# Three VectorE operations of a graph-attention kernel take one operand from PSUM instead of SBUF

## The chip, the cores and the metric

The kernel runs on one core of a Trainium2 chip. A core has five engines with a queue of instructions each: TensorE (PE), which multiplies 128 x 128 tiles and writes to PSUM; VectorE (DVE) and ScalarE (ACT), which work on 128 partitions at a time and reach SBUF and PSUM; GpSimd (POOL), which here issues the gathers and scatters whose row numbers lie in SBUF; and SyncE (SP), which issues plain transfers. Engines wait for each other through semaphores. The metric is the device time of one execution in microseconds (us). The kernel before took 1271.98 us, the median of three runs (1270.6 to 1276.46).

## The reference

6250 nodes with 256 features, 100,000 edges (src, dst), two attention heads of 128 features. The layer norm of the features is projected, each edge gets a weight, the weighted rows of the destinations are summed by source, and a feed-forward layer follows in which each row goes to the one expert of eight that its gate likes best:

```python
Wh = (x @ W_w + W_b).reshape(N, H, D)              # x: layer norm of the input
s = jnp.einsum('nhd,d->nh', Wh, a_src); t = jnp.einsum('nhd,d->nh', Wh, a_dst)
e = jax.nn.leaky_relu(s[src] + t[dst], negative_slope=0.2)
m = jax.ops.segment_max(e, src, num_segments=N)
ex = jnp.exp(e - m[src])
alpha = ex / jax.ops.segment_sum(ex, src, num_segments=N)[src]
agg = jax.ops.segment_sum(alpha[:, :, None] * Wh[dst], src, num_segments=N)
h_prime = jnp.where(deg[:, None, None] > 0, agg, Wh)
...
x = x + h_prime                                    # first residual
H = jax.nn.gelu(xf @ W1 + b1, approximate=False)   # xf: layer norm of x
probs = jax.nn.softmax(H @ Wg + bg); assign = jnp.argmax(probs, axis=-1)
out = x + probs[assign] * (H @ Wd[assign] + bd[assign])
```

## The kernel before

It works in a prelude and 49 blocks of 128 nodes (`NB`), the last of 106.

**Prelude, 0 to about 115 us.** Each partition gets 784 edges as keys made of source and destination, and VectorE sorts them (`exchange`, L290). Between the steps of the sort VectorE takes the layer norm's statistics, TensorE projects the nodes, and ScalarE writes a row of 260 numbers for each node to `table` in HBM: two heads of 128 features with the terms of the attention. The bias `Wb` is loaded to 128 partitions (L246). `hot_terms` (L491) takes the attention terms of the first 256 nodes, the "counted destinations", from `hot_x` into `hot_e`; edges to these nodes are not gathered but counted per pair of source and destination.

**Blocks.** A block takes three slots of time, and the work of several blocks overlaps. `at(slot, place, fn)` collects all work in a plan, and the sorted plan is the order in which every engine's queue is filled; no scheduler changes it. For block b with u = 3b, the pieces that matter here are:

- `window` (L615): POOL fetches the block's sorted keys. `measure` and `split` (L625, L657) on VectorE take counts, row numbers (`dsti`) and places from them. `split` has the two long operations that make `pick` (L662, L663).
- `pick_pairs` (L677), slot u-2, place 62.758: four comparisons (L681) make `dests`; L682 compares the row numbers 128 to 255, read from the bf16 tile `iota_bf`, with `place_i` and makes `places`, 128 x 512 bf16. TensorE multiplies the two into the counts of pairs (L691).
- `fetch` (L788), slots u to u+2, place 30: POOL gathers the rows of 5, 5 and 4 edges per partition, each in one indirect DMA of 128 rows (L792). The row number of each partition is read from `dsti` in SBUF. The tile `wg` has five buffers.
- `compare_back` (L806), slots u+1 to u+3, place 51.259: VectorE compares `iota_ps` with `loc` and makes the one-hot tile `hot` (L809). `iota_ps` holds the numbers 128 to 255 in fp32 in the PSUM tile `fix`.
- `weigh` (L814), slots u+2 to u+4, place 8.751: VectorE makes the factors (L821, L822), puts them into columns 128 to 183 of `fix`, multiplies the gathered rows for one head by them (L823); ScalarE copies the factors from `fix` (L824) and weighs the other head (L826).
- `add_up` (L828), slots u+3 to u+5: TensorE sums the gathered rows by source (L833).
- `scale_terms` on ScalarE (L704) and `weigh_pairs` on VectorE (L706), slot u+2, place 51: L709 takes the maximum of `wt` and one half of `hot_e`, and L710 multiplies by the counts in PSUM.
- `owned` and `owned_biased` (L797, L802), slots u+5 and u+6: the block's own rows of x are loaded, and L804 adds the bias to them. `finish` (L840) adds the sums of the edges.

Four blocks at a time go through the first half of the feed-forward layer (L920), are sent by POOL to lists by expert (L1064), and full tiles of a list come back for the second half (L1154). After the last block a tail of such tiles follows.

`fix` fills one PSUM bank of 512 fp32 columns: `iota_ps` in 0 to 127, the factors in 128 to 183, and nothing in the rest. VectorE writes and reads it, ScalarE reads it at L824. The planner of semaphores puts accesses of two engines to one PSUM bank in order, also where both read.

Of the kernel before, what the change touches and what calls it, by code (L numbers as in the profile page):

```python
# [10 lines left out]
F32 = mybir.dt.float32  # L11
# [3 lines left out]
AF = mybir.ActivationFunctionType  # L15
# [8 lines left out]
P = 128  # L24
# [12 lines left out]
def common_path(  # L37
# [22 lines left out]
    nc = tc.nc  # L60

    N, C = x.shape
    E = src.shape[0]
    HC = W.shape[1]
    D = a.shape[0] // 2
    H = HC // D
# [13 lines left out]
    HB, HK = 2, 4  # L80
# [5 lines left out]
    T = ND + NC  # L86
# [4 lines left out]
    D2 = D + H  # L91
    TW = H * D2
    SE = D2 + D
# [17 lines left out]
    const = ctx.enter_context(tc.tile_pool(name="const", bufs=1))  # L111
# [50 lines left out]
    iota_bf = const.tile([P, HOT], BF16, name="iota_bf")  # L162
    nc.vector.tensor_copy(iota_bf, iota_s[:, :HOT])

    hot_x = const.tile([P, HB, TW], F32, name="hot_x")
    hot_e = const.tile([P, HB, 2, H], F32, name="hot_e")
    cnt = const.tile([P, NB], F32, name="cnt")
    late = const.tile([P, NB, 3], F32, name="late")
    den_all = const.tile([P, NB, H], F32, name="den_all")
    nc.gpsimd.memset(den_all, 1.0)  # L170
    bad = const.tile([P, 4], F32, name="bad")

    bias = const.tile([P, C], F32, name="bias")
    src_term = const.tile([P, NB, H, 3], BF16, name="src_term")

    def rows_of(b):
        return min(P, N - b * P)
# [16 lines left out]
    with ExitStack() as edges:  # L194
# [3 lines left out]
        def at(slot, place, fn, *args):  # L198
            plan.append((slot, place, len(plan), fn, args))
# [9 lines left out]

        fix = pfix.tile([P, 512], F32, name="fix")  # L210
        iota_ps = fix[:, :P]
        nc.vector.tensor_scalar(iota_ps, iota_r, float(P), None, op0=ALU.add)

        pre = ExitStack()
        sp = pre.enter_context(tc.tile_pool(name="sort", bufs=1))
# [3 lines left out]
        def early(t, fn, *args):  # L219

            at((t - TG) / TS, 0, fn, *args)
# [21 lines left out]
                                in_=W[:, h * D:(h + 1) * D].rearrange("(k p) c -> p k c", p=P))  # L243
        a_bc = sp.tile([P, 2 * D], F32, name="a_bc")
        nc.scalar.dma_start(out=a_bc, in_=a.partition_broadcast(P))
        nc.scalar.dma_start(out=bias, in_=Wb.partition_broadcast(P))  # L246

        keya = sp.tile([P, KQ * P], F32, name="keya")
# [241 lines left out]

        def hot_terms():  # L491
            for g in range(HB):
                nc.vector.tensor_copy(hot_e[:, g], hot_x[:, g, :].rearrange("p (a c) -> p a c", a=2)[:, :, D:])
            nc.vector.memset(hot_x[:, :, D:D2], 1.0)

        def node_terms():
# [9 lines left out]
        early(0.25, make_keys)  # L506
        early(0.3, columns, KC)
        early(0.32, bias_terms)
        early(7, keep_gaps)
        NODE, XN0 = 1.6, 9.0  # L510
        for i, (d, flip) in enumerate(steps):
# [17 lines left out]
        for f0, f1, t0, step in ((n0, n1, 8.0, 0.7), (n4, NB - 1, 15, 2.0)):  # L529
            for j, b in enumerate(range(f0, f1)):  # L530
                c = b % CH
# [24 lines left out]
        early(TG - 0.5, node_terms)  # L556
        early(70, load_hot)
        early(76, hot_terms)


# [41 lines left out]
        wt = {}  # L602
# [10 lines left out]
        win, kept, rows, own, sums, res = {}, {}, {}, {}, {}, {}  # L613
# [63 lines left out]
        def pick_pairs(b):  # L677
            pair, place_i = kept[b].pop("pair"), kept[b].pop("place")
            d, p = kept[b]["both"] = [kp.tile([P, HK, w], BF16, name=n, bufs=1) for n, w in (("dests", HOT), ("places", P))]
            for r in range(HK):  # L680
                nc.vector.tensor_scalar(d[:, r, :], iota_bf, pair[:, r:r + 1], None, op0=ALU.is_equal)  # L681
            nc.vector.tensor_tensor(p, iota_bf[:, P:2 * P].unsqueeze(1).to_broadcast([P, HK, P]),  # L682
                                    place_i[:, :HK].unsqueeze(2).to_broadcast([P, HK, P]), op=ALU.is_equal)

        def count_pairs(b):
# [13 lines left out]
        def scale_terms(b, g):  # L699
            tm = kept[b]["tm"]  # L700
            if g == 0:
                kept[b]["wt"] = ep.tile([P, HB, H, P], F32, name="wt", bufs=2)
            for h in range(H):
                nc.scalar.activation(kept[b]["wt"][:, g, h, :], tm[:, h, :], AF.Identity, scale=hot_e[:, g, 1, h:h + 1])  # L704

        def weigh_pairs(b):  # L706
            kept[b].pop("tm")
            wt = kept[b]["wt"]
            nc.vector.tensor_max(wt, wt, hot_e[:, :, 0, :].unsqueeze(3).to_broadcast([P, HB, H, P]))  # L709
            nc.vector.tensor_mul(wt, wt, kept[b].pop("pc").unsqueeze(2).to_broadcast([P, HB, H, P]))  # L710

        def add_pairs(b):
# [88 lines left out]

        def owned_biased(b):  # L802
            r = rows_of(b)
            nc.vector.tensor_add(own[b][:r], own[b][:r], bias[:r])  # L804

        def compare_back(b, q):  # L806
            hot = ep.tile([P, HT, P], F32, name="hot", bufs=4)
# [390 lines left out]
        for b in range(NB):  # L1198
            u = 3 * b
            at(u + -6, 64.258, window, b)  # L1200
            at(u + -4, 24, measure, b)
            at(u + -4, 50.755, prefix, b)
            at(u + -3, 5, prefix_out, b)
            at(u + -3, 12, split, b)
            at(u + -3, 33.7, gather_late, b)
            at(u + -2, 62.758, pick_pairs, b)
            at(max(u + -1, -0.2), 63, load_terms, b)
            at(u + 1, 18.756, scale_terms, b, 0)
            at(u + 2, 4.751, scale_terms, b, 1)
            at(u + 0, 51.019, count_pairs, b)  # L1210
            at(u + 2, 51, weigh_pairs, b)
            at(u + 4, 51.256, add_pairs, b)
            at(u + -2, 16, choose, b)
            at(u + -2, 33.5, spread, b)
            at(u + 0, 9, compare, b)
            at(u + 0, 33, factors, b)
            at(u + 1, 47, factor_sums, b)
            at(u + 5, 42.752, owned, b)
            at(u + 6, 13, owned_biased, b)
            for q in range(3):  # L1220
                at(u + 0 + q, 30, fetch, b, q)
                at(u + 1 + q, 51.259, compare_back, b, q)
                at(u + 2 + q, 8.751, weigh, b, q)
                at(u + 3 + q, 32, add_up, b, q)
            at(u + 6, 14, finish, b)
# [3 lines left out]
        for k in range(NPH):  # L1229
# [19 lines left out]
            for i in range(len(bs)):  # L1249
                t, p = (((v + 6, 40), (v + 6, 41), (v + 8, 60), (v + 8, 61))[i] if last else  # L1250
                        ((v + 10, 38), (v + 11, 38), (v + 12, 21.26), (v + 13, 57.754))[i])
# [34 lines left out]
@with_exitstack  # L1286
def gat_then_ffn_kernel(
    ctx: ExitStack,
    tc: tile.TileContext,
    x: bass.AP,  # L1290
    src: bass.AP,
    dst: bass.AP,
    W: bass.AP,
    Wb: bass.AP,
    a: bass.AP,
    W1: bass.AP,
    b1: bass.AP,
    Wg: bass.AP,
    bg: bass.AP,
    Wd: bass.AP,  # L1300
    bd: bass.AP,
    out: bass.AP,
):
    keep = ctx.enter_context(tc.tile_pool(name="keep", bufs=1))
    odd = keep.tile([1, 1], I32, name="odd")
    common_path(tc, x, src, dst, W, Wb, a, W1, b1, Wg, bg, Wd, bd, out, odd)
    flag = tc.nc.values_load(odd[0:1, 0:1], min_val=0, max_val=1,
                             skip_runtime_bounds_check_because="a flag, 0 or 1")
    with tc.If(flag > 0):
        general_path(tc, x, src, dst, W, Wb, a, W1, b1, Wg, bg, Wd, bd, out)  # L1310
# [506 lines left out]
```

## Time and profile before

| | |
|---|---|
| time of three runs | 1270.6, 1271.98, 1276.46 us |
| the profiled execution's own time | 1270.99 us |
| its span, first to last instruction | 1268.9 us |
| outside the span | 2.1 us |
| mean granted TensorE clock | 0.948 of full speed |
| PE busy | 1108.0 us (87%) |
| VectorE busy | 969.4 us (76%) |
| POOL busy | 835.5 us (66%) |
| ScalarE busy | 677.6 us (53%) |
| gathers (L792) | 686, mean 981 ns |
| L682, L709, L804 on VectorE | 49 of each, mean 681, 685 and 418 ns |

Busy time is the time in which an engine carries out instructions; what it waits for, and what it needs between two instructions, is not in it. The view by line gives for a group of instructions the busy time, the mean duration, the idle time of the engine just before them and what ended it ("issue" where no wait of the profile ended just then). The view of windows gives busy times for a stretch of the span. A timeline row begins with the start in us from the span's start and the duration in us.

### The profile page before, as it was taken

What the parts mean: (1) busy time and instruction counts of PE and PEld (TensorE: products, weight loads), DVE (VectorE), ACT (ScalarE), POOL (GpSimd) and SP (SyncE); (2) the same over time, 40 slices, a digit from 0 to 9 for tenths busy, and PEclk for the clock granted to TensorE, in tenths of its full rate; (3) what the DMA queues carried; (4) which work ended last, traced back from release to release, by engine and by line L of the source; (5) the groups of instructions that cost most, each with busy time, mean ns of one, the idle gap of its engine ahead of it and who ended that gap; (6) DMA issues with size and microseconds to landing.
All of it is one profiled execution on the core that took longest, in us unless ns stands there. A gap on an engine that the chain in (4) does not pass through costs nothing.

```text
span 1268.9 us, 22698 instructions
## 1 busy us (share of the span) xinstructions
PE 1108.0 (87%) x6551; PEld 864.0 (68%) x6551; DVE 969.4 (76%) x3509; ACT 677.6 (53%) x2011; POOL 835.5 (66%) x941
## 2 busy tenths in 40 slices
PE   4685677697888989999989999999999999999994
PEld 3464565566566677786876867868678687685784
DVE  6986889888979789798897997979979979753110
ACT  4684344555646447556474665655745647555221
POOL 1003777777777777777777777777777777736551
PEclk9797688898998989999999999999999999999998
DMA  4764776656555666666766666575667566747860
GB/s 142 220 196 137 200 199 207 192 190 200 173 173 176 218 172 214 190 223 197 216 191 217 212 195 206 183 241 177 222 187 227 183 211 187 230 138 298 318 202 13
DMA packets 115977, 249.77 MB, mean 197 GB/s; under 512 B 23372, under 2 KB 69656, under 8 KB 115702
## 3 DMA queue, kind: packets, MB, share of 16 engines
q0 software_dynamic: 44192, 131.04, 33.3%
q1 hardware_dynamic: 64342, 110.14, 27.3%
q10 hardware_dynamic: 7312, 7.05, 1.7%
q8 instruction: 56, 0.92, 0.3%
q14 instruction: 75, 0.61, 0.2%
HBM read 196.90 MB, written 57.97 MB: 201 GB/s over the span
## 4 chain that ended last, share of the span: by engine, by line
PE 42%; DVE 25%; DMA 12%; ACT 10%; issue 5%; POOL 4%; SPq 0%; ACTq 0%; DVEq 0%; POOLq 0%
PE pf L1154 11%; PE p_a L833 10%; PE pf L920 9%; DMA wg<-table,dsti 7%; POOL wg L792 3%; DVE wg L823 3%; PE pm L738 3%; DVE hot L809 3%; PE pf L1043 2%; ACT wg L826 2%; DMA lbc<-lrow 2%; DVE pick L663 2%; PE pf L456 1%; PE p_a L717 1%; DVE dests L681 1%
## 5 line engine op out<-in xcount | busy, mean ns | idle before, releaser
L792 POOL DMA_INDIRECT wg<-table,dsti x686 | 672.8, 981 | 211.4 <-issue 162.5
L833 PE MATMUL p_a<-wg,hot 128*128 128x258 f32 x1372 | 339.8, 396 | 0.0
L833 PEld LDWEIGHTS p_a<-wg,hot 128*128 128x128 f32 x1372 | 265.9, 198 | 57.4 <-issue 17.9
L826 ACT ACTIVATE wg<-wg 128x128 f32<-128x128 f32 x686 | 216.7, 390 | 4.8
L1154 PE MATMUL pf<-wd_sb,half 128*128 x880 | 205.6, 387 | 1.1
L1154 PEld LDWEIGHTS pf<-wd_sb,half 128*128 128x128 f32 x880 | 163.3, 191 | 31.4 <-ACT half L1044 5.5
L920 PE MATMUL pf<-xT,w_sb 128*128 128x512 f32 (+1 forms) x416 | 182.4, 584 | 0.5 <-ACT xT L912 0.5
L824 ACT COPY wg<-fix 128x10 f32<-128x10 f32 x147 | 24.1, 164 | 224.9 <-DVE wg L823 188.6
L920 PEld LDWEIGHTS pf<-xT,w_sb 128*128 128x128 f32 x416 | 75.3, 196 | 73.3 <-issue 69.2
L1044 ACT COPY half<-pf 128x512 f32<-128x512 f32 x110 | 59.1, 588 | 115.2 <-PE pf L1043 115.2
L823 DVE TENSOR_TENSOR wg<-wg,fix 128x640 f32<-128x640 f32 x147 | 114.1, 776 | 5.1
L809 DVE TENSOR_TENSOR hot<-fix,loc 128x640 f32<-128x640 f32 x147 | 112.7, 767 | 0.0
L738 PE MATMUL pm<-rest,pick 128*128 128x33 f32 x588 | 82.3, 295 | 15.1 <-DVE place_i L666 15.0
L738 PEld LDWEIGHTS pm<-rest,pick 128*128 128x128 f32 x588 | 77.8, 211 | 16.0 <-ACT wg L826 9.8
L922 ACT ACTIVATE hT<-pf,b_sb 128x512 f32<-128x512 f32 (+1 forms) x104 | 65.7, 655 | 29.4 <-PE pf L920 28.3
L456 PE MATMUL pf<-w_sb,xT 128*128 128x260 f32 x196 | 61.6, 443 | 19.1 <-ACT xT L450 19.0
L1064 POOL DMA_INDIRECT by_expert<-row,place_i x47 | 48.4, 1030 | 37.4 <-ACT row L1059 19.9
L704 ACT ACTIVATE wt<-tm,hot_e 128x128 f32<-128x128 f32 x196 | 67.8, 395 | 0.0
L619 POOL DMA_INDIRECT win<-keys,first x49 | 46.9, 958 | 28.9 <-DMA keys<-keyb 12.0
L821 DVE TENSOR_TENSOR fe<-fs,wg 128x10 f32<-128x10 f32 x147 | 24.1, 164 | 53.9 <-DMA wg<-table,dsti 50.1
L1043 PE MATMUL pf<-ident,hT 128*128 128x128 f32 x392 | 54.4, 278 | 10.7 <-ACT row L1044 5.4
L456 PEld LDWEIGHTS pf<-w_sb,xT 128*128 128x128 f32 x196 | 38.6, 219 | 28.7 <-ACT xT L450 24.3
(273 smaller groups left out, 1800.1 us busy)
## 6 DMA issues: line engine op xcount, KB each, us to landing
row<-by_expert SPq DMA_DIRECT2D x39, 641.0 KB
lbc<-lrow SPq DMA_DIRECT2D x49, 448.0 KB
wg<-table,dsti POOLq DMA_INDIRECT x686
wg<-by_expert SPq DMA_DIRECT2D x16, 641.0 KB
wd_sb<-in_L_ffn_Wd_dram SPq DMA_DIRECT2D x8, 1024.0 KB
tm<-terms SPq DMA_DIRECT2D x49, 128.0 KB
table<-tb ACTq DMA_DIRECT2D x12, 520.0 KB
xs<-in_x_dram SPq DMA_DIRECT2D x12, 512.0 KB
```

Of the source, the lines that this page charges most:

```text
L456: nc.tensor.matmul(pW[:, :TW], xT[:, k * P:(k + 1) * P], w_sb[:, k, :], start=(k == 0), stop=(k == KC - 1))
L704: nc.scalar.activation(kept[b]["wt"][:, g, h, :], tm[:, h, :], AF.Identity, scale=hot_e[:, g, 1, h:h + 1])
L738: nc.tensor.matmul(pk[:, c, :], k["pick"][:, c * P:(c + 1) * P], k["rest"], start=True, stop=True)
L792: nc.gpsimd.indirect_dma_start(out=wg[:, t - QS[q], :], out_offset=None, in_=table[:, :], in_offset=bass.IndirectOffsetOnAxis(ap=kept[b][" ...
L809: nc.vector.tensor_tensor(hot[:, :n], iota_ps.unsqueeze(1).to_broadcast([P, n, P]), kept[b]["loc"][:, QS[q]:QS[q + 1]].unsqueeze(2).to_bro ...
L823: nc.vector.tensor_mul(wg[:, :, :D], wg[:, :, :D], p_w[:, :, 0:1].to_broadcast([P, n, D]))
L826: nc.scalar.activation(wg[:, t, D2:SE], wg[:, t, D2:SE], AF.Identity, scale=wg[:, t, D + 1:D2])
L833: nc.tensor.matmul(sums[b], hot[:, t - QS[q], :], wg[:, t - QS[q], :SE], start=(t == 0), stop=(t == T - 1))
L920: nc.tensor.matmul(ph[:, :w], wt["w1"][:, k, j * P:(j + 1) * P], xT[:, k, :w], start=(k == 0), stop=(k == KC - 1))
L922: nc.scalar.activation(hT[:, j, :w], ph[:, :w], AF.Gelu, bias=wt["b1"][:, j:j + 1])
L1043: nc.tensor.transpose(pT[:, j * P:(j + 1) * P], rows(4 * h + j), ident)
L1154: nc.tensor.matmul(py[:, :C], res[k]["half", i, j // 4][:, j % 4, :], wt["wd"][:, ds(of * KH + j * C, C)], start=False, stop=(j == KH - 1))
```

## The change

The free columns of `fix` take two more constants. Columns 184 to 187 become `hot_ps`, the one half of the counted destinations' terms; columns 256 to 511 become `bias_ps`. Then:

- L682 reads `iota_ps` (fp32, PSUM) in place of the upper half of `iota_bf` (bf16, SBUF). Its other input, `place_i`, and its output stay in SBUF.
- L709 reads `hot_ps` in place of `hot_e[:, :, 0]`.
- L804 reads `bias_ps` in place of `bias`.
- `hot_terms` makes four copies of 128 x 2 in place of two of 128 x 4; two of them go to PSUM.
- A copy of 128 x 256 from `bias` to `bias_ps` is added to the prelude, just after `bias_terms`; the SBUF tile `bias` is given up after the prelude.

The instructions of the other engines and their order are the same. On VectorE two waits for ScalarE move or appear: in the slots that have L709, the wait for ScalarE's read of `fix` (L824) that stood at L809 stands at L709, two operations earlier; and L804 waits for L824 too, which it did not.

```diff
+        hot_ps = fix[:, P + 2 * T * H:P + 2 * T * H + HB * H].rearrange("p (g h) -> p g h", h=H)
+        bias_ps = fix[:, 512 - C:]
...
             for g in range(HB):
-                nc.vector.tensor_copy(hot_e[:, g], hot_x[:, g, :].rearrange("p (a c) -> p a c", a=2)[:, :, D:])
+                nc.vector.tensor_copy(hot_ps[:, g], hot_x[:, g, D:D2])
+                nc.vector.tensor_copy(hot_e[:, g], hot_x[:, g, SE:])
...
         early(0.32, bias_terms)
+        early(0.33, lambda: nc.vector.tensor_copy(bias_ps, bias))
...
-            nc.vector.tensor_tensor(p, iota_bf[:, P:2 * P].unsqueeze(1).to_broadcast([P, HK, P]),
+            nc.vector.tensor_tensor(p, iota_ps.unsqueeze(1).to_broadcast([P, HK, P]),
                                     place_i[:, :HK].unsqueeze(2).to_broadcast([P, HK, P]), op=ALU.is_equal)
...
-            nc.vector.tensor_max(wt, wt, hot_e[:, :, 0, :].unsqueeze(3).to_broadcast([P, HB, H, P]))
+            nc.vector.tensor_max(wt, wt, hot_ps.unsqueeze(3).to_broadcast([P, HB, H, P]))
...
-            nc.vector.tensor_add(own[b][:r], own[b][:r], bias[:r])
+            nc.vector.tensor_add(own[b][:r], own[b][:r], bias_ps[:r])
```

More of the change, by code (lines that the diff above doesn't have):

```diff
@@ L165, in common_path @@
     hot_x = const.tile([P, HB, TW], F32, name="hot_x")
-    hot_e = const.tile([P, HB, 2, H], F32, name="hot_e")
+    hot_e = const.tile([P, HB, H], F32, name="hot_e")
     cnt = const.tile([P, NB], F32, name="cnt")
@@ L171, in common_path @@
     bad = const.tile([P, 4], F32, name="bad")
-    bias = const.tile([P, C], F32, name="bias")
     src_term = const.tile([P, NB, H, 3], BF16, name="src_term")
@@ L245, in common_path @@
         nc.scalar.dma_start(out=a_bc, in_=a.partition_broadcast(P))
+        bias = sp.tile([P, C], F32, name="bias")
         nc.scalar.dma_start(out=bias, in_=Wb.partition_broadcast(P))
@@ L703, in scale_terms @@
             for h in range(H):
-                nc.scalar.activation(kept[b]["wt"][:, g, h, :], tm[:, h, :], AF.Identity, scale=hot_e[:, g, 1, h:h + 1])
+                nc.scalar.activation(kept[b]["wt"][:, g, h, :], tm[:, h, :], AF.Identity, scale=hot_e[:, g, h:h + 1])
         def weigh_pairs(b):
```

## The prediction

> **What bounds the kernel now.** I read the busy times by window first, then POOL's waits, then the gathers' line, then timeline rows in which two engines meet.
>
> The page gives PE 87% and POOL 66%, which makes POOL look idle. The windows (length, then busy time and count of PE, PE's weight loads, VectorE, ScalarE and POOL, then clock, DMA share and GB/s) say how steady the blocks are:
>
> ```profile
> 115.00:320.00 205.00, 149.42 (x925) 118.96 (x925) 169.04 (x597) 92.19 (x307) 156.93 (x160) 0.82 0.65 193
> 520.00:720.00 200.00, 191.92 (x1222) 151.92 (x1221) 169.36 (x611) 113.58 (x335) 153.22 (x161) 0.99 0.66 207
> 920.00:1116.00 196.00, 189.03 (x1192) 147.72 (x1191) 161.29 (x577) 113.24 (x333) 149.71 (x157) 1.00 0.65 205
> ```
>
> POOL is busy about 153 us in 200 and carries out about 160 instructions in each. Its waits from 130 to 1110 us (total, times, longest) show what fills the rest:
>
> ```profile
> POOL wg L792 <- issue: 158.5, 520, 0.3
> POOL wg L792 <- DMA wg<-table,dsti: 10.4, 34, 0.3
> POOL wg L792 <- PE p_a L833: 8.8, 29, 0.3
> ```
>
> No gap before a gather is longer than 0.3 us, whoever is named, and nearly every gather has one: 158.5 / 520 = 0.30. It is a fixed cost between two of them, not a wait. 160 x 0.30 = 48 us, and 153 + 48 = 201 of 200: POOL works back to back from 115 to 1116 us. One gather costs 0.945 + 0.30 = 1.25 us. The gathers' own line tells the rest (min/median/max in ns, and who waited for them):
>
> ```profile
> L792 POOL DMA_INDIRECT wg<-table,dsti x686: 942/949/1497, 114.9 to 1116.3; - x172
> ...
>   DVE fe L821: 50.1, 18
>   ACT wg L824: 26.3, 8
> ```
>
> The consumers run up against the gathers 26 times, for 76 us; the times of these waits lie between 211 and 1089 us, the last one (ScalarE) 5.4 us long at 1089. PE and VectorE fall behind while a feed-forward group passes (the chain that ended last is then on PE), then catch up and wait for a gather's landing. So POOL's issue sets the pace of the 1001 us of blocks; PE, 192 of 200 in the middle, is close behind.
>
> **What holds a gather.** The median is 949 ns and the mean on the page 981. The timeline around 428 us (start, us):
>
> ```profile
> 428.08 0.68 DVE L682 TENSOR_TENSOR places<-iota_bf,place_i 128x512 bf16<-128x512 bf16 x1
> 428.12 1.48 POOL L792 DMA_INDIRECT wg<-table,dsti  x1 [0.30 <-issue]
> ...
> 430.76 0.68 DVE L709 TENSOR_TENSOR wt<-wt,hot_e 128x512 f32<-128x512 f32 x1
> 431.16 1.10 POOL L792 DMA_INDIRECT wg<-table,dsti  x1 [0.30 <-issue]
> ```
>
> The first gather starts 0.04 us after L682 and ends at 429.60, which is 0.84 us after L682's end (428.76). The second starts under L709 and ends at 432.26, 0.82 us after L709's end (431.44). Both behave as if the last 0.83 us could begin only when the VectorE operation was over: about 0.11 us after its start a gather needs something, its row numbers in SBUF I think, that the operation keeps from it.
>
> I counted this in the trace: for each of POOL's 839 indirect DMAs, which VectorE operation runs 130 ns after its start, and what the DMA takes above 945 ns. All excess is 31.1 us. Under L682: 25 DMAs, 6.6 us. Under L709: 25 DMAs, 5.1 us. Under L663 (two SBUF inputs, unchanged): 21, 6.7 us. Under L804: nothing, its place in the slot misses the reads. Under L809 (99 DMAs) and L710 (22), which read one operand from PSUM: 4 and 6 ns each, nothing. So an operation of the same size with one PSUM operand does not hold a gather, and that is what the change makes of L682 and L709.
>
> **The change part by part.**
>
> **1. Gathers released.** 6.6 + 5.1 = 11.7 us less POOL time. As a check from sizes: a 0.68 us operation meets a reading in 0.68 / 1.25 = 54% of 49 cases, that is 27, for 0.34 us on average, 9 us each; the trace has 25 and 25 and less per case. [...]
> A freed gather's successors start earlier and may run into L663, L662 or L771, which still hold. The unchanged holders cost 31.1 - 11.7 = 19.4 us in 1001, 2% of the time, so 0.2 us of 11.7 by chance; since POOL and VectorE are not independent I take 1.0. PE's nearness takes a tenth, 1.0. Left: 9.7 us, all on the path.
>
> **2. The operations' own time.** Rows of VectorE (busy, mean ns, idle before):
>
> ```profile
> L710 DVE TENSOR_TENSOR wt<-wt,pm 128x512 f32<-128x512 f32 x49 | 33.6, 686 | 1.7
> L709 DVE TENSOR_TENSOR wt<-wt,hot_e 128x512 f32<-128x512 f32 x49 | 33.6, 685 | 6.8 <-ACT wg L824 3.3 <-ACT wt L704 3.2
> L682 DVE TENSOR_TENSOR places<-iota_bf,place_i 128x512 bf16<-128x512 bf16 x49 | 33.3, 681 | 0.0
> L809 DVE TENSOR_TENSOR hot<-fix,loc 128x512 f32<-128x512 f32 x49 | 32.8, 670 | 0.0
> ```
>
> L710 takes 686 with an operand in PSUM where L709 takes 685 without; L809 is what L682 becomes but for the output's type, 670 against 681. L804 (128 x 256, 418 ns) has a pair of half its size: L747 from SBUF 359, L749 from PSUM 354. Sum: 49 x (-11 + 1 - 5) ns = -0.7 us. [...]
>
> **3. Prelude.** VectorE is busy without a break from 18 to 104 us there, and all else waits for the sorted keys, so its additions are on the path. The copy of 128 x 256 to PSUM: nearest are 0.39 for a 128 x 224 copy (L284) and 0.37 for a 128 x 256 cast (L163); 0.4. Two more small copies: a COPY of 128 x 4 is 179 ns (L1000), some 0.1 of it overlapped, and one new wait on VectorE itself; 0.25 (between 0.15 and 0.5). Sum +0.65.
>
> **4. Waits.** L709 now waits until ScalarE has done L824, which until now was asked two operations later. In the trace ScalarE was done 0.64 us ahead of L709 in the median; in 9 of 49 cases it was not done 60 ns ahead, in all 1.0 us short. For L804 the lead is 1.8 us or more except twice, 0.35 us short in all. Behind the waiting L709 on VectorE's queue stand L710, L809 and the next slot's L821 to L823, and for these TensorE waits with the sums of the pairs (L717) and of the gathered rows (L833). VectorE idles 31 of 200 us, so 1.35 us is covered; without the cover it is +1.35. I take 0.
> Row numbers for the gathers (L753) come from VectorE two slots ahead, so POOL does not wait for it.
>
> **Sum.** -9.7 + 0.65, and -0.7 of VectorE hidden: -9.0 us. From the profiled execution: 1271.0 - 9.0 = 1262.0. The median of the three runs is 1.0 above the profiled one, which would give 1263; the lowest run is 0.4 below it. I say 1262.5.
>
> **Rivals.** A measurement of this kernel tells about 0.5%, 6.4 us, from no change: faster means below 1265.6, slower above 1278.3.
> - **PE takes the pace.** From 520 us on PE is busy 192 in 200. If it were the real floor there, the gathers' gain after 520 (60% of 11.7, 7.0 us) would be lost, and 4.7 - 0.65 = 4 us stays: 1268. For it: long stretches of PE in the chain after 870. Against: consumers still wait 5.4 us for a gather at 1089, and 198 us per 200, which the gain asks for, is above 192.
> - **The change doesn't release the gathers**, because what holds them is not the second SBUF operand, or they run into L663 instead: 0 + 0.65, 1272.6. Against: L809 and L710 hold nothing.
> - **ScalarE's wait on L709 becomes the bound.** ScalarE's queue also has the feed-forward's 0.65 us activations in front of L824. If POOL's lead shrinks and L824 comes later in the slot, VectorE stands at L709 in each of 49 blocks. A block is 20.4 us with 3.2 of VectorE idle; a stall decides only beyond 3.2. With a stall of 3.5 us in each block VectorE sets the pace, the gathers' gain lies hidden behind it, the path grows by 0.3 x 49 = 15, and with the prelude the end is 1272.0 + 15 + 0.65 = 1287.6. Against: the shortfall today is 1.0 us in all.
>
> **Chances.** Forecast 0.70; PE takes the pace 0.13; nothing released 0.10; ScalarE's wait 0.07. Of the forecast 0.02 ends above 1265.6, and of the PE case 0.04 below: faster 0.68 + 0.04 = 0.72, same 0.02 + 0.09 + 0.10 = 0.21, slower 0.07. Range: the forecast's own is 1257 (all of 11.7 and 3 us more by better phase) to 1267; with the PE case and part of the third, 1256 to 1271.
>
> **What would show it.** Right: gathers' mean falls from 981 to about 966 ns, POOL's busy time by 11 us, the last gather starts at about 1107 in place of 1116.3; L682, L709 and L804 within 15 ns of before; no gathers above 1.1 us under L682 or L709; idle before L709 below 9 us. Wrong if the mean stays near 981 (not released, or L663 takes them), if POOL's gaps exceed 0.3 (it waits for others: PE), or if idle time before L709 grows by tens of us.

## The result and the profile after

The changed kernel takes 1262.02 us (median of 6 runs, 1261.49 to 1263.06), the kernel before 1271.34 beside it (6 runs, 1270.1 to 1276.46). The ratio is 0.9924, with a 95% interval from 0.9903 to 0.9945: faster by 0.55 to 0.97%. The forecast was 1262.5. The profiled execution of the changed kernel took 1262.07 us with a span of 1260.0, against 1270.99 and 1268.9 before, so the two traces differ by 8.9 us. Five of the experiments below ran on chips on which the kernel before itself takes 1690 to 1724 us, at a granted clock of 0.84 to 0.86 (0.94 to 0.96 elsewhere); they stand apart, at the end.

In the block part the line numbers are 4 higher than before: L682 is now L686, L709 is L713, L804 is L808, and the gathers are L796. The page of the changed kernel, busy times and the gathers' row:

```profile
PE 1102.2 (87%) x6551; PEld 861.3 (68%) x6551; DVE 968.5 (77%) x3512; ACT 677.1 (54%) x2011; POOL 828.1 (66%) x941
...
L796 POOL DMA_INDIRECT wg<-table,dsti x686 | 664.1, 968 | 209.0 <-issue 172.1
```

The mean of a gather has gone from 981 to 968 ns. POOL is busy 7.4 us less, VectorE 0.9 us less; PE, at a granted clock of 0.953 in place of 0.948, is busy 5.8 us less. The clock is not what made the kernel faster: the six executions of the changed kernel have 0.946 to 0.953, and the one at 0.946 is the fastest of them, 1261.49 us; 26 executions of the kernel before beside the first experiments have 0.943 to 0.955 and take 1267.5 to 1276.2. The gathers' own line (min/median/max in ns, first and last start in us) and who waits for them:

```profile
L796 POOL DMA_INDIRECT wg<-table,dsti x686: 942/946/1454, 114.5 to 1106.0; - x172
...
  ACT wg L828: 45.4, 12
  DVE fe L825: 44.5, 22
```

The last gather starts at 1106.0 us in place of 1116.3. The consumers still run up against the gathers, 34 times for 90 us, so POOL's issue still sets the pace. Its waits from 130 to 1103 us (total, times, longest) say the same, with nothing above the fixed 0.3 us in front of a gather:

```profile
POOL wg L796 <- issue: 168.5, 553, 0.3
POOL wg L796 <- DMA wg<-table,dsti: 7.6, 25, 0.3
...
POOL wg L796 <- PE p_a L837: 7.0, 23, 0.3
```

The timeline around 611 us shows the two places at which the prediction's first view of the mechanism stood (start and duration in us). A gather that starts 0.27 us into L686, and one that starts together with L713, each take 0.95 us. Had they ended 0.83 us after the operation's end, as the held ones did before, they would have taken 1.24 and 1.51:

```profile
611.15 0.68 DVE L686 TENSOR_TENSOR places<-fix,place_i 128x512 bf16<-128x512 f32 x1
611.42 0.95 POOL L796 DMA_INDIRECT wg<-table,dsti  x1 [0.30 <-issue]
...
613.92 0.95 POOL L796 DMA_INDIRECT wg<-table,dsti  x1 [0.30 <-issue]
613.92 0.68 DVE L713 TENSOR_TENSOR wt<-wt,fix 128x512 f32<-128x512 f32 x1
```

The changed operations by shape (busy us, mean ns, idle before):

```profile
L714 DVE TENSOR_TENSOR wt<-wt,pm 128x512 f32<-128x512 f32 x49 | 33.7, 687 | 1.7
L713 DVE TENSOR_TENSOR wt<-wt,fix 128x512 f32<-128x512 f32 x49 | 33.4, 681 | 6.0 <-ACT wg L828 5.8
L686 DVE TENSOR_TENSOR places<-fix,place_i 128x512 bf16<-128x512 f32 x49 | 33.3, 680 | 0.0
...
L808 DVE TENSOR_TENSOR own<-own,fix 128x256 f32<-128x256 f32 x48 | 20.2, 421 | 3.5 <-DMA own<-in_x_dram 3.3 <-ACT wg L828 0.2
```

They cost what they cost before (681, 685 and 418 ns), and the two waits for ScalarE come to 5.8 us at L713 and 0.2 us at L808.

**Where the 8.9 us went.** From the first gather's start to the last one's end POOL carries out 774 indirect DMAs. I split that length into 774 x 0.945 = 731.4 us, the DMAs' excess over that (the holds), the memsets, and the gaps between instructions. The numbers come from the instructions' times in each trace; us:

| | first gather | length | holds | memsets | gaps | span |
|---|---|---|---|---|---|---|
| before | 114.9 | 1002.3 | 28.8 | 4.0 | 238.0 | 1268.9 |
| after | 114.5 | 992.5 | 21.2 | 4.5 | 235.3 | 1260.0 |

The length falls by 9.8: 7.6 from the holds and 2.7 from the gaps, less 0.5 at the memsets. The start is 0.4 earlier, the tail after the last gather 1.3 longer; 9.8 + 0.4 - 1.3 = 8.9.

And the holds by what ran on VectorE 130 ns after a DMA's start (all 839 indirect DMAs; how many met the operation, how many of these took more than 1.02 us, and their excess over 0.945 us in all):

| VectorE's operation | before | after |
|---|---|---|
| places (L682, L686) | 25, 17, 6.6 us | 31, 0, 0.4 us |
| terms (L709, L713) | 25, 22, 5.1 us | 29, 0, 0.05 us |
| second operation of pick (L663, L667), unchanged | 21, 15, 6.7 us | 23, 20, 9.0 us |
| lbc (L771, L775), unchanged | 21, 5, 1.6 us | 25, 12, 4.5 us |
| everything else | 11.1 us | 9.6 us |
| all | 31.1 us | 23.5 us |

More gathers than before meet the two changed operations, and none is held. 11.2 us were released, and 5.3 us more than before were spent under pick and lbc.

The ends of the DMAs say the same in another way. All 39 that took more than 1.02 us under L682 and L709 end 0.82 to 0.86 us after that operation's end, as the two in the prediction's timeline do.

Two large inputs in SBUF are not all that holds, though. lbc (L771, L775) and the first operation of pick (L662, L666) are unchanged and have one large input each, with one number per partition as the second operand. They hold too: 8 of 19 DMAs took more than 1.02 us under L662, and 13 of 23 under L666. And lbc also holds the last part of a DMA that began before it. The rows are from the changed kernel:

```profile
822.45 1.24 POOL L796 DMA_INDIRECT wg<-table,dsti  x1 [0.30 <-issue]
822.88 0.68 DVE L775 TENSOR_SCALAR lbc<-lbc,iota_p 128x1792 bf16<-128x1792 bf16 x1
```

The gather ends at 823.69, 0.12 us after lbc. 12 DMAs do so before and 17 after, for 2.3 and 3.2 us, which the table counts under what ran at 130 ns ("everything else"). Such holds at the end are not seen with L682 and L709: 44 DMAs began 0.2 to 0.8 us ahead of one of these two and still ran when it did, and none took more than 1.02 us. Why one large input is enough in these two operations and not in L681 (128 x 256; before, 31 DMAs met it and none took more than 1.02 us) is open; so is what the DMA waits for, its row numbers being the prediction's guess.

### The profile page after: what moved, and what is told of

Its sections match the earlier page's. It is cut to its first block, busy times and chain, and to the rows that moved or that the text cites. A ratio compares the mean times of both kernels' runs of the same rounds, so it can differ in the third digit from the quotient of the medians.

```text
span 1260.0 us, 22750 instructions
## 1 busy us (share of the span) xinstructions
PE 1102.2 (87%) x6551; PEld 861.3 (68%) x6551; DVE 968.5 (77%) x3512; ACT 677.1 (54%) x2011; POOL 828.1 (66%) x941
## 4 chain that ended last, share of the span: by engine, by line
PE 46%; DVE 23%; DMA 10%; ACT 8%; issue 5%; POOL 5%; SPq 1%; ACTq 0%; DVEq 0%; POOLq 0%
PE pf L1158 12%; PE p_a L837 11%; PE pf L924 10%; POOL wg L796 4%; DMA wg<-table,dsti 4%; PE pm L742 4%; DVE wg L827 3%; PE pf L1047 3%; DVE hot L813 2%; PE p_a L721 2%; PE pf L962 2%; ACT wg L830 1%; DVE pick L667 1%; DVE dests L685 1%; ACT hT L926 1%
## 5 line engine op out<-in xcount | busy, mean ns | idle before, releaser
L796 POOL DMA_INDIRECT wg<-table,dsti x686 | 664.1, 968 | 209.0 <-issue 172.1
L828 ACT COPY wg<-fix 128x10 f32<-128x10 f32 x147 | 24.0, 163 | 212.4 <-DVE wg L827 163.7
L813 DVE TENSOR_TENSOR hot<-fix,loc 128x640 f32<-128x640 f32 x147 | 112.7, 767 | 0.0
L742 PEld LDWEIGHTS pm<-rest,pick 128*128 128x128 f32 x588 | 76.1, 207 | 14.9 <-ACT wg L830 9.4
L1047 PE MATMUL pf<-ident,hT 128*128 128x128 f32 x392 | 54.4, 278 | 10.7 <-ACT row L1048 5.4
L825 DVE TENSOR_TENSOR fe<-fs,wg 128x10 f32<-128x10 f32 x147 | 23.7, 161 | 45.4 <-DMA wg<-table,dsti 44.5
L1048 ACT COPY row<-pf 128x512 f32<-128x512 f32 x94 | 50.6, 582 | 13.8 <-PE pf L1047 13.5
```

What stands on the lines that cost most here:

```text
L742: nc.tensor.matmul(pk[:, c, :], k["pick"][:, c * P:(c + 1) * P], k["rest"], start=True, stop=True)
L796: nc.gpsimd.indirect_dma_start(out=wg[:, t - QS[q], :], out_offset=None, in_=table[:, :], in_offset=bass.IndirectOffsetOnAxis(ap=kept[b][" ...
L813: nc.vector.tensor_tensor(hot[:, :n], iota_ps.unsqueeze(1).to_broadcast([P, n, P]), kept[b]["loc"][:, QS[q]:QS[q + 1]].unsqueeze(2).to_bro ...
L1047: nc.tensor.transpose(pT[:, j * P:(j + 1) * P], rows(4 * h + j), ident)
L1048: nc.scalar.copy(o, pT)
```

## The experiments

My theory: an indirect DMA on POOL is held while VectorE runs an operation with both large inputs in SBUF (whatever else may hold it); the change takes that from two operations, and POOL's issue sets the pace, so the time follows. The rivals: the bias, or the operands' type, makes the difference; what holds is not the memory; or POOL does not set the pace any more.

### One part at a time

**Only the places.** The kernel before, with L682 alone changed:

```diff
-            nc.vector.tensor_tensor(p, iota_bf[:, P:2 * P].unsqueeze(1).to_broadcast([P, HK, P]),
+            nc.vector.tensor_tensor(p, iota_ps.unsqueeze(1).to_broadcast([P, HK, P]),
```

> The kernel before with one line changed: the places are compared with row numbers from PSUM. Theory (a second SBUF operand holds the gathers): the 6.6 us that gathers took too long under this operation go, the other holders stay and take about a third of that back, as they did in the whole change; 1271.3 - 4.4 = 1267, the operation itself 680 ns as before, no gather above 1.1 us under it. Rival (the gain comes from moved waits or from the prelude, which this kernel leaves alone): 1271.

Measured: 1265.64 us (6 runs) beside 1272.27 (26 runs), ratio 0.9943 (0.9925 to 0.9961), that is -6.6 us. In its trace 25 gathers meet L682 and their excess is 0.30 us in all (6.6 before); 24 meet L709, which still has two inputs in SBUF, and lose 5.4. The sum of the holds in POOL's stretch is 24.4 us, 4.4 below before, and the gaps are 3.5 us shorter. This one edit has most of the gain, and it leaves the prelude and the two moved waits alone, so these don't make it.

**Only the terms.** The kernel before with `hot_ps`, its copies and L709 alone (here L711):

```diff
+        hot_ps = fix[:, P + 2 * T * H:P + 2 * T * H + HB * H].rearrange("p (g h) -> p g h", h=H)
...
-            nc.vector.tensor_max(wt, wt, hot_e[:, :, 0, :].unsqueeze(3).to_broadcast([P, HB, H, P]))
+            nc.vector.tensor_max(wt, wt, hot_ps.unsqueeze(3).to_broadcast([P, HB, H, P]))
```

> The kernel before with the counted destinations' terms in PSUM alone. Theory: 5.1 us of held gathers go, a third comes back, 0.3 us for two more copies in the prelude; 1271.3 - 3.1 = 1268. Rival (moved waits): this is the operation whose wait for ScalarE moves ahead, so it has either the whole gain of 9 us, 1262, or a loss of up to 1.4 us, 1272.7. Rival (no effect of PSUM): 1271.6.

Measured: 1270.2 us (8 runs), ratio 0.999 (0.9973 to 1.0007): -2.1 us, and not told from no change. The mechanism is there all the same: 24 gathers meet L711 with 0.01 us of excess, against 20 of 24 held under the places (6.1 us). But pick's second operation holds 10.1 us in this trace and lbc 4.3, so the holds in all fell by only 1.8 us.

**Only the bias.** The kernel before with `bias_ps`, its copy in the prelude and L804 alone:

```diff
+        early(0.33, lambda: nc.vector.tensor_copy(bias_ps, bias))
...
-            nc.vector.tensor_add(own[b][:r], own[b][:r], bias[:r])
+            nc.vector.tensor_add(own[b][:r], own[b][:r], bias_ps[:r])
```

> The kernel before with the bias in PSUM alone, with its copy in the prelude and its new wait for ScalarE. Theory: no gather was held under this operation, so nothing is won, and the copy costs 0.4 us; 1271.7. Rival (any operation with two SBUF inputs costs in proportion to its time, 418 ns against 681): a gain of about 3 us, 1268.

Measured: 1272.8 us (11 runs), ratio 1.0005 (0.9988 to 1.0022): nothing, as the theory has it for an operation that one DMA met in the kernel before, without being held. This trace is the most useful control of all. Nothing is released in it, and yet its holds are 37.1 us against 31.1 before: pick 11.1 where before had 6.7, lbc 5.0 where it had 1.6, places and terms 6.6 and 6.7 where they had 6.6 and 5.1. Its profiled execution took 1276.1 us, 3.3 above its own median. So the holds differ by 6 us between two kernels where nothing was done to the holders, I think by how VectorE's and POOL's sequences lie to each other; each kernel has one trace, so two executions of one kernel can't be compared.

The parts add to -6.6 - 2.1 + 0.5 = -8.2 us; the whole gave -9.3. The difference is within the parts' intervals.

### Memory or type

L682 did not only change its memory: it had read bf16, and reads fp32 now. This kernel is the changed one, with L686 reading the same numbers as fp32 from SBUF:

```diff
-            nc.vector.tensor_tensor(p, iota_ps.unsqueeze(1).to_broadcast([P, HK, P]),
+            nc.vector.tensor_tensor(p, iota_s[:, P:2 * P].unsqueeze(1).to_broadcast([P, HK, P]),
```

> The changed kernel, but the places are compared with fp32 row numbers in SBUF: type as after, memory as before. Theory: the gathers are held under it again, 4.4 us lost, 1262 + 4.4 = 1266.5, some 25 gathers over 1.02 us under it. Rival (the type of the operand, bf16 against fp32, made the difference): 1262, no such gathers.

Measured: 1270.98 us (12 runs), ratio 0.9984 (0.9971 to 0.9997). The holds are back with the memory, and the time with them. From the timeline around 680 us, where a gather starts 0.27 us into L686, as it did at 611 us in the changed kernel:

```profile
679.75 0.67 DVE L686 TENSOR_TENSOR places<-iota_s,place_i 128x512 bf16<-128x512 f32 x1
680.02 1.22 POOL L796 DMA_INDIRECT wg<-table,dsti  x1 [0.30 <-issue]
```

The gather ends at 681.24, 0.82 us after L686's end. 17 of the 20 gathers that met it took more than 1.02 us, 5.4 us of excess. For the hold the type does not matter, the memory does. I had expected 1266.5, too low: what is left in this kernel is the terms' and the bias's part, and these two alone gave -1.6 us.

### More of the suspected cost

`compare_back` (L813) is VectorE's operation that meets most gathers, some 95 of them, and it reads `iota_ps` from PSUM before and after. If two SBUF inputs are what holds, moving it to SBUF must bring holds that neither kernel has. The changed kernel with:

```diff
-            nc.vector.tensor_tensor(hot[:, :n], iota_ps.unsqueeze(1).to_broadcast([P, n, P]),
+            nc.vector.tensor_tensor(hot[:, :n], iota_s[:, P:2 * P].unsqueeze(1).to_broadcast([P, n, P]),
```

> The changed kernel with the one-hot comparison (147 operations of 0.77 us) from SBUF again, on a chip on which the kernel before takes 1272 us, since on the one of the first look it took 1724 us. There the gathers were held for 23.4 us under this operation, and the time did not show it, because POOL waited for ScalarE and TensorE. Theory here: 25 to 35 us more of held gathers than after the change, 1287 to 1297. Rival (the memory of an operand does not matter, or the hold is always absorbed): 1262 to 1265.

Measured: 1283.53 us (5 runs) beside 1270.83 (24 runs), ratio 1.0086 (1.0056 to 1.0115). Against the changed kernel's 0.9924 that is 1.6% more, some 20 us, for one operand. The timeline around 541 us, and the operation's and the gathers' rows (busy us, mean ns, idle before):

```profile
541.00 0.82 DVE L813 TENSOR_TENSOR hot<-iota_s,loc 128x640 f32<-128x640 f32 x1
541.07 1.57 POOL L796 DMA_INDIRECT wg<-table,dsti  x1 [0.30 <-issue]
```

```profile
L813 DVE TENSOR_TENSOR hot<-iota_s,loc 128x640 f32<-128x640 f32 x98 | 80.2, 819 | 0.0
```

```profile
L796 POOL DMA_INDIRECT wg<-table,dsti x686 | 685.2, 999 | 209.0 <-issue 166.4 <-DMA wg<-table,dsti 8.8 <-PE p_a L837 7.9
```

The gather ends at 542.64, 0.82 us after L813's end at 541.82, the distance that the prediction read off two other operations. 73 of 93 gathers are held, for 26.8 us (none, 0.4 us, with the operand in PSUM), and all 73 end 0.81 to 0.86 us after L813's end. The operation itself takes 819 ns, as from PSUM (815 to 821). I had expected 34 us of holds and 1287 to 1297; the direction and place are right, the holds are four fifths of that, and the time lies 3.5 us below the range.

### Does POOL still set the pace

With PE at 192 of 200 us in the middle of the span, the changed kernel could have come to PE's limit. This kernel gives POOL 49 memsets of 128 x 256 to a tile that nothing reads, each before the first gather of a block:

```diff
+    pad = const.tile([P, 256], F32, name="pad")
...
             wg = gp.tile([P, HT, TW], F32, name="wg")
+            if q == 0:
+                nc.gpsimd.memset(pad, 0.0)
```

> The changed kernel with one memset of 128 x 256 on GpSimd ahead of the first gather of each block, where the kernel before takes 1272 us. Theory (POOL still sets the pace): the time rises by what POOL takes longer, about 0.25 x 49 = 12 us, to 1274. Rival (TensorE sets the pace after the change): 1262 to 1265.

Measured: 1273.72 us (20 runs), ratio 1.0017 (1.0003 to 1.0031); the changed kernel at 0.9924 of 1270.83 would be 1261.2, so the memsets cost 12.5 us. The added line, then POOL's waits (from 130 to 1103 us):

```profile
L796 POOL MEMSET pad<- x49: 325/335/737, 114.1 to 1104.9; 128x256 f32 x49
```

```profile
POOL wg L799 <- issue: 163.3, 552, 0.3
POOL wg L799 <- DMA wg<-table,dsti: 8.2, 27, 0.3
```

In the accounting of the first table: memsets +18.8 us, gaps -7.6, holds +4.8, the start 0.1 later, the tail 1.2 shorter: the span grows by 14.8 (1260.0 to 1274.8; this profiled execution is 2.9 us above the median of its kernel). A memset of 0.335 us costs some 0.23 us, since (18.8 - 7.6) / 49 = 0.23; the rest is in the gaps, 7.6 us shorter. The 77 small memsets (1 x 1) of the kernel before show such shorter gaps: each begins within 0.04 us of the end of the DMA ahead, and the next DMA starts 0.23 us after it in the median, where a DMA right behind a DMA starts 0.305 us after it. What the memsets add on POOL, 11.2 us net, comes out at the end. PE does not take the pace. The page alone would not have said so: its chain of the work that ended last puts 46% of the changed kernel's span on PE and 5% on POOL.

### Further on: pick from PSUM

After the change the largest holder is pick's second operation. `fix` has room for all 768 row numbers as 16-bit integers (384 columns), if the bias goes back to SBUF. In this kernel, pick's second operation (L669) and `hit` (L753) read them from there, and so do L688 and `hot` (the two operations in the prelude that put the numbers there are not shown):

```diff
-        iota_ps = fix[:, :P]
+        words = P * NC // 2
+        iota_all = fix[:, :words].bitcast(U16)
+        iota_ps = iota_all[:, P:2 * P]
...
-            nc.vector.scalar_tensor_tensor(pick, iota_s, late[:, b, 2:3], pick, op0=ALU.is_lt, op1=ALU.mult)
+            nc.vector.scalar_tensor_tensor(pick, iota_all, late[:, b, 2:3], pick, op0=ALU.is_lt, op1=ALU.mult)
...
-            nc.vector.tensor_tensor(hit, iota_s[:, :NR].unsqueeze(1).to_broadcast([P, NC, NR]),
+            nc.vector.tensor_tensor(hit, iota_all[:, :NR].unsqueeze(1).to_broadcast([P, NC, NR]),
...
-            nc.vector.tensor_add(own[b][:r], own[b][:r], bias_ps[:r])
+            nc.vector.tensor_add(own[b][:r], own[b][:r], bias[:r])
```

> The changed kernel with the second operation of the pick and the comparison that finds a late edge's number reading from PSUM, as 16-bit integers; the bias is back in SBUF. On the two slower chips (kernel before at 1690 to 1720 us) the holds fell to 13.7 us in the trace, against 21.2 after the change, but POOL waited 420 us for ScalarE and others, so that the time could not show it. Theory, on a chip where the kernel before takes 1271 us: 7.5 us of holds less than after the change and no copy of the bias in the prelude, 1262 - 7.9 = 1254. Rival (TensorE, busy 192 of 200 us, has become the bound): 1260 to 1263. If the chip is again a slow one: no difference from the kernel before beyond 2%.

Measured: 1268.5 us (22 runs) beside 1273.19 (27 runs), ratio 0.997 (0.9955 to 0.9984). It is a miss: 14.5 us above what I expected, and slower than the changed kernel. The holds did go: 37 gathers meet L669 with 0.7 us of excess, and the holds in POOL's stretch fall to 14.8 us from 21.2, although the bias's operation, back in SBUF, holds 17 of the 19 gathers that meet it, for 2.4 us (in the kernel before one DMA met it: it lies elsewhere in POOL's sequence). But POOL now waits for others, and VectorE waits less for gathers and more for the rest of the work. POOL's waits, then VectorE's, from 130 to 1110 us:

```profile
POOL by_expert L1070 <- ACT row L1050: 10.7, 6, 3.2
...
POOL by_expert L1070 <- ACT rest L661: 4.2, 1, 4.2
```

```profile
DVE lbc L777 <- DMA lbc<-lrow: 24.2, 14, 3.5
DVE fe L827 <- DMA wg<-table,dsti: 10.7, 6, 4.4
DVE hit L753 <- ACT wg L830: 8.8, 35, 0.5
```

POOL's waits beyond the fixed gap are 16.1 us (4.3 in the changed kernel), most of them for rows that ScalarE had still to make before POOL could send them. VectorE's waits at `fe` for gathers fall from 44.5 to 10.7 us, and in their place it waits at lbc for its data (24.2, from 10.4), at `col` for TensorE (27.5, from 19.9) and, newly, at `hit` for ScalarE's read of `fix`: 8.8 us in 35 places. So 6.4 us fewer holds, with 12 us more of waiting, and a span 7.6 us longer than the changed kernel's. What set the end here was no longer POOL's issue alone. Pick and `hit` were not tried apart where the kernel before takes 1272 us, so how much of the loss is `hit`'s new wait, and whether pick alone would have gained, stays open. No version tried beats the changed kernel.

### Runs that say little

The same edits as above, `hot` from SBUF and the memsets, where the kernel before takes 1724.42 us (1684 to 1745):

> The changed kernel, but the one-hot tile of each slot is compared with row numbers from SBUF, 147 operations of 0.77 us. Theory: each meets a gather's reading in 0.77 / 1.25 = 61% of cases for 0.38 us on average, 34 us of held gathers, less where holders overlap; POOL sets the pace, so the time rises by 25 to 35 us, to 1287 to 1297, at an unchanged duration of the operation. Rival (the memory of an operand does not matter to the gathers): 1262. Rival (TensorE sets the pace): POOL has slack and less than 10 us show.

> The changed kernel with one memset of 128 x 256 on GpSimd ahead of the first gather of each of the 49 blocks; nothing reads it. A memset of this size took 0.31 to 0.36 us. Theory (POOL still sets the pace): the time rises by what POOL takes longer, some 0.25 us x 49 = 12 us, to 1274. Rival (TensorE sets the pace after the change): POOL has slack, under 3 us show, 1263 to 1265.

Measured: 1696.85 and 1734.75 us, both inside the spread of the kernel before. POOL's waits in the kernel with `hot` from SBUF show why neither need say anything:

```profile
POOL wg L796 <- issue: 215.2, 590, 6.3
POOL by_expert L1068 <- ACT row L1063: 142.2, 21, 14.9
POOL wg L796 <- ACT wg L828: 76.5, 14, 9.7
```

The holds are there, 41.8 us in POOL's stretch of this trace (23.4 of them under `hot`), but POOL waits 402 us for others, up to 14.9 at a time. A hold of 0.4 us in front of such a wait may vanish in it, which was not shown. This is the same kernel that lost 20 us where POOL set the pace; the changed kernel itself was not timed here, so what the holds cost here is not known.

Pick from PSUM without `hit` (all of the edit above but `hit`'s lines), there and where the kernel before takes 1689.4 us, and with `hit`, at the second place:

> The changed kernel with the next holder released: the second operation of the pick reads the numbers 0 to 767 from PSUM as 16-bit integers, the row numbers of the other comparisons come from the same place, and the bias goes back to SBUF. Theory: the 9.0 us of held gathers under that operation go, a third comes back, 1262 - 6 = 1256, if the operation still takes about 1.02 us. Rival (TensorE has become the bound): 1260 to 1262. Rival (16-bit integers from PSUM are slower to read): the comparison and the pick take longer and the time is above 1262.

> The changed kernel with the next holder released: the second operation of the pick reads 0 to 767 from PSUM as 16-bit integers, and the bias is back in SBUF. On the first, slower chip its operations kept their times and the holds under the pick went from 9 us to nothing. Theory: with POOL setting the pace, 9 us go, a third comes back: 1256. Rival (TensorE has become the bound): 1260 to 1263.

> The same, and the comparison that finds a late edge's number (128 x 192) reads from PSUM too. Theory: 1.6 us of holds more go (the figure of the first chip's trace): 1255. Rival (TensorE has become the bound): the same as without it.

Measured: 1717.52 beside 1724.42, then 1681.9 beside 1689.4 (ratio 1.0117, 1.0025 to 1.0209, which goes the other way than the medians, since it rests on two of the eleven executions of the kernel before, which range from 1641 to 1699), and 1697.19 beside 1689.4 (1.0194, 1.0116 to 1.0273). Both of these are unclear. POOL waits some 390 to 430 us for others in all three. They don't tell pick's part from `hit`'s.

## Why the prediction was right

**1. Gathers released: the mechanism is right, one term was mis-sized, and the other had the wrong sign.** Of the 11.7 us counted under L682 and L709, 11.2 went, and the same two places hold no gather in the changed kernel; the places in fp32 and `hot` from SBUF show that it is the second input's memory. With both large inputs in SBUF, L682, L709, L686 in the type experiment and L813 held 17 of 25, 22 of 25, 17 of 20 and 73 of 93 of the DMAs that met them (over 1.02 us); with one in PSUM L686 and L713 held none of 31 and of 29.

The term that was mis-sized is "successors may run into L663, L662 or L771 ... I take 1.0". Unchanged operations took 3.7 us more (23.1 after, 19.4 before), with 5.3 more at pick and lbc and 1.6 less elsewhere. The working took "2% of the time by chance" from the trace of before, as if its 19.4 us were a property of the kernel. Six experiments' traces can be set beside it (pick reads SBUF in them, and the kernel before takes about 1272 us there). In these, all operations but the places, the terms and, where it was moved, `hot` hold for 21.2 to 28.1 us; pick's second operation alone holds for 9 to 13, where before had 6.7. The bias experiment, which released nothing, is one of them, with 23.9. So it was not shown that the freed gathers themselves ran into pick: the trace of before had the least of all, and one trace can't give that term to better than some 4 us.

"PE's nearness takes a tenth, 1.0" had the wrong sign in the accounting: POOL's gaps shrank by 2.7 us, of which 2.1 or 2.2 are waits beyond the fixed gap (6.5 to 4.3 us). The memsets show that PE takes nothing yet. But such waits come to 3.3 to 7.8 us in the same six traces, so these 2 us are not shown to come from the change. The errors nearly cancel, which is why the 9.7 us came out at that size: 11.2 released, less 3.7 at other holders, less 0.5 at memsets, and 2.7 of gaps. That the sum came so close is luck; that POOL got its time back from the two operations is not.

**The share of each part** was put at 6.6 to 5.1, by the holds. The places alone gave 6.6 us, the terms alone 2.1 with an interval that holds zero.

**2. The operations' own time.** 681 to 680, 685 to 681 and 418 to 421 ns, forecast -11, +1 and -5: within 15 ns, and nothing in the sum. A PSUM source costs at most 3 ns more at any of the three, and nothing at `hot`, 819 ns from SBUF and 815 to 821 from PSUM. That VectorE hides the 0.7 us, as the sum has it, no run shows; it is busy 0.9 us less in the whole span.

**3. Prelude.** The copy to `bias_ps` takes 0.42 us in the trace (forecast 0.4). VectorE, which the prediction saw busy without a break from 18 to 104 us, has 79.6 us of busy time in those 86 and one pause of 2.6. The copies' effect can't be seen: the first gather starts at 114.5 us, 0.4 earlier than before, and between 114.5 and 117.5 in the kernels of this study, so the 0.65 us lies within that spread.

**4. Waits.** The idle time before L713 is 6.0 us, where L709 had 6.8, and its part from ScalarE's copy 5.8, where it was 3.3; the wait for the row `wt` (L704, 3.2) is no longer named, and most of it seems to have gone into the wait for L828. L808 waits 0.2 us for ScalarE. The value taken, 0, is right, and so the rival on the slower side, which needed 3.2 us in each block, is out by far: 6.0 us in 49 blocks is 0.12 in each.

**The rivals.** "PE takes the pace" is refuted by the memsets: 12.5 us more for work that was added on POOL alone. "Nothing is released" is refuted by the table of holds. **The signals** were: mean of a gather about 966 ns (968), last gather at about 1107 (1106.0), no gather over 1.1 us under the two operations (none over 1.02), idle before L709 below 9 us (6.0). One missed: POOL's busy time was to fall by 11 us and fell by 7.4, for the reason under 1.

## What to carry to other kernels

Where an engine shows a low busy share but its gaps are all of one length, add that length to each of its instructions before calling it idle: POOL at 66%, with 0.30 us before each gather, was full, and time put on it came out at the end (12.5 us for 11.2). Time taken off it came out too (9.3 us, for 9.8 less in POOL's stretch), until others were waited for: pick from PSUM took 6.4 us of holds off and lost. Then look at which operations of other engines run while its long instructions run long; that operations of the same size with one operand in PSUM held nothing (L809: 99 DMAs, none over 1.02 us, 0.4 us of excess in all) was in the trace of before, and made the forecast possible. One trace gives what is released where the cause is removed, but not what the unchanged holders will take afterwards: compare several traces for that. And look at what an operand in a shared PSUM bank makes its reader wait for (`hit`: 35 of 49 blocks, 0.25 us on average).

## What was not expected of the hardware

- Of the differences between traces in what unchanged operations hold, nothing is seen in VectorE's own rows: pick's second operation took 1018 or 1019 ns in all that were compared above. The hold shows only in the gathers' durations.
- A 16-bit integer operand in PSUM cost VectorE no more than fp32 in SBUF: 1018 ns for 128 x 768 both ways, and 358 for 360 at `hit`.
- An operation with one large input held DMAs as one with two did (over 1.02 us: 13 of 23 under L666 and 12 of 25 under lbc, beside 20 of 23 under L667), and lbc holds its last part too (12 and 17 DMAs, 0.12 us after its end), which none of the operations with two SBUF inputs that the experiments moved was seen to do.
- A memset of 128 x 256 takes 0.335 us on POOL in the median and cost 0.23: with 49 of them POOL's gaps were 7.6 us shorter.
